# Mixing experts on sixteen small array tiles, loading one image's planes at another place, and a new order in layer 3's first steps

## The chip, the cores and the metric

One Trainium2 chip, and one of its cores. The metric is the device time of one execution in microseconds. A core has a matrix engine (TensorE, PE in the profile, with PEld for its weight loads), a vector engine (VectorE, DVE), a scalar engine (ScalarE, ACT), GpSimd (POOL) and SyncE (SP), which here only starts transfers; sixteen DMA engines move data between the chip's memory (DRAM) and the on-chip memories. TensorE writes its sums into PSUM, eight banks of 128 partitions x 512 fp32 values. Everything is fp32, and TensorE handles each fp32 product in two passes: the profile shows two records for each.

## The reference

Four layers on eight images of 512 channels and 32x32 positions. Layer 0: group norm, eight-head attention, three steps of `h += 0.1*tanh(W h + b)`, a projection and a residual. Layer 1: single-head self-attention with a residual. Layer 2: up- and downsampling with a leaky ReLU between. Layer 3, where most of the change lies, mixes eight sets of expert weights per image and runs a bottleneck with them:

```python
pooled = x.mean(axis=(2, 3))
rw = jax.nn.sigmoid(pooled @ router_w.T + router_b)      # 8 gates for each image
W  = jnp.einsum('be,eoihw->boihw', rw, experts)          # the image's own weights
out = relu(bn(conv1x1(x, W1)));  out = relu(bn(conv3x3(out, W2)))
out = relu(bn(conv1x1(out, W3)) + x)
```

## The kernel before

All 128-row operands are kept as tiles of 128 partitions. Large products are done by seven half-size products (P1, C11, U2, U3, C22, C21, C12), whose operands are sums of quarters made by VectorE (`quarter_sums`). `product` runs them with the banks A in a small PSUM pool and X, Y in the pool `ps_sc`, two buffers of two banks; `in_turn` runs the same seven with one output half after the other, in three banks of the small pool.

The images run one after the other through layers 0 to 2; an image's layer 2 is interleaved with the next image's first products. The last image, number 7, has no next one: beside its layer 2 the kernel runs layer 3 of images 0 and 1 (`lean_images`), a generator named `chain` from which one step is taken at each `fill()`. Images 2 to 7 follow in the main loop of layer 3.

**The early experts.** The gates of images 0 to 6 are known before image 7's layer 0 ends, so `blend_early` mixes their weights there. The experts are laid out as 128 rows (16 groups of 8 experts) by 17,408 columns, cut into 34 pieces of 512. `operators` puts the gates into a block-diagonal 128x128 operand (the rows of `ident`, grouped by `here`, times the gates); each piece is one 128x128x512 product (L310), copied out of PSUM by ScalarE (L316) and stored by GpSimd's queue (L317) in the DRAM tensor `mixed`. One piece is taken at each of the seven parts of the last two inner steps, and three at each part of the last projection. `load_weights` (L1504) reads an image's weights back from there in three loads of 128 rows; `mixed_of` (L236) finds the rows.

**Where the order comes from.** Attention, `last_across`, `last_rows`, `last_columns` and the main loop of layer 3 stand in sections whose order is as written for TensorE, VectorE and ScalarE (in the `last_` ones for SP too). The end of layer 0 with the mixing, and layer 1, are ordered by a scheduler. Each engine takes its instructions in the order that results, and SP its transfers.

**Layer 2 of image 7.** `wide` (L1232) makes columns, stored through `across` and read back as `turned` (`turn`); `fine_passes` runs `up(n)` (L1262), two scaled copies by ScalarE (L1268) and two maxima by VectorE (L1269), then `down(n-1)` (L1280, copies to `sent` L1286, stores `back_u` L1289), and two fills; `turn_back`, `narrow` and `channels` follow. `load_z(1)` (L1466), image 1's planes, stands behind `turn(1)` in `last_across`.

**Layer 3.** `first` is the 1x1 convolution c1 (L1631) and its ReLU into `rim`; `spread` makes sums of its columns; `second` runs c2 (L1573) and c3 (L1667), whose result VectorE adds to the image's planes (L1670), ScalarE finishes (L1673) and SP stores. `transform_weights` turns the 3x3 weights into sums, one ScalarE operation (L1521) and three on VectorE (L1522 to L1524) an image. `blend_last` mixes image 7's weights beside the main loop.

Wide temporary tiles (`tmp` with 1024 columns) rotate through six buffers, `big_tile` through seven.

Of the kernel before, what the change touches and what calls it, by code (L numbers as in the profile page):

```python
# [36 lines left out]
NR = P // NE  # L37
WE = NE * WX
# [19 lines left out]
def tile_sequence(ctx: ExitStack, tc: tile.TileContext, a: dict, out: bass.AP, shifted: bool):  # L58
# [156 lines left out]
    def late_loads():  # L215
# [10 lines left out]
        "early": const.tile([P, B, NR], F32, name="blend_early"),  # L226
# [3 lines left out]
    nc.gpsimd.memset(blend["early"], 0.0)  # L230
    mixed = {
        "early": spill.tile([EARLY * NR, WE], F32, name=f"mixed_{run}", tag="mixed"),
# [3 lines left out]
    def mixed_of(b):  # L236
        rows = mixed["last"] if b == EARLY else mixed["early"][ts(b, NR), :]
        return rows.rearrange("g (p c) -> (g p) c", c=WX)

    class Router:  # L240
# [34 lines left out]
        def operator(self, to):  # L275
            for _ in self.operators(to):
                pass

        def operators(self, to):
            here = ident.rearrange("p (g e) -> p g e", e=NE)  # L280
            for b in range(self.n):
                t = tmp(f"here_{self.name}_{b}")[:, 0:P].rearrange("p (g e) -> p g e", e=NE)
                gate = rw[:, self.images, :][:, b, :].unsqueeze(1).to_broadcast([P, NR, NE])
                nc.vector.tensor_tensor(t, here, gate, ALU.mult)
                nc.vector.tensor_reduce(to[:, b, :], t, AX.X, ALU.add)
                yield

    PIECES = WE // HALF
    BLOCK = CC * S // HALF

    def blend_early():
        rows = EARLY * NR
        op = blend["early"].rearrange("p b g -> p (b g)")
        tiles = []

        def load():
            at = len(tiles) * BLOCK * HALF
            n = min(BLOCK * HALF, WE - at)
            if n > 0:
                t = big_tile(f"experts_{len(tiles)}", [P, BLOCK * HALF])  # L300
                nc.sync.dma_start(t[:, 0:n], a["experts"][:, at : at + n])
                tiles.append(t)

        for _ in range(2):
            load()
        yield
        for i in range(PIECES):
            ps = bank(ps_tp, f"mix_{i}")
            n, at = divmod(i, BLOCK)
            nc.tensor.matmul(  # L310
                ps, op, tiles[n][:, ts(at, HALF)], start=True, stop=True
            )
            if at == BLOCK - 1:
                load()
            t = tmp(f"mix_{i}")
            nc.scalar.copy(t[0:rows, :], ps[0:rows, :])  # L316
            nc.gpsimd.dma_start(mixed["early"][:, ts(i, HALF)], t[0:rows, :])  # L317
            yield

    def blend_last():  # L320
        per = -(-PIECES // 4)
# [3 lines left out]
        def load(t):  # L325
            tiles[t] = big_tile(f"last_experts_{t}", [P, 4, 2 * HALF])
            for c in range(4):
                n = min(2, per - 2 * t, PIECES - per * c - 2 * t)
                if n > 0:
                    at = (per * c + 2 * t) * HALF  # L330
                    nc.sync.dma_start(
                        tiles[t][:, c, 0 : n * HALF], a["experts"][:, at : at + n * HALF]
                    )

        def counts(t):
            return [max(0, min(2, per - 2 * t, PIECES - per * c - 2 * t)) for c in range(4)]

        n_tiles = -(-per // 2)
        load(0)
        yield  # L340
        for t in range(n_tiles):
# [4 lines left out]
            for i in range(2):  # L346
# [12 lines left out]
                if i == counted[0] - 1:  # L359
                    for c in range(4):  # L360
                        n = counted[c] * HALF
                        at = (per * c + 2 * t) * HALF
# [449 lines left out]
    def early_router():  # L812
        router = Router(0, EARLY)
        router.sums()
        yield
        router.logits()
        router.gates()
        yield
        yield from router.operators(blend["early"])

    def layer0(b, q, k, v, w):
# [202 lines left out]
        for it in (1, 2):  # L1024
# [189 lines left out]
    class Layer2:  # L1214
# [37 lines left out]
        def up(self, e, i):  # L1252
# [88 lines left out]
        def fine_passes(self, fill=lambda: None):  # L1341
            order = [(e, i) for e in range(2) for i in range(4)]
            for n in range(len(order) + 1):
                if n < len(order):
                    self.up(*order[n])
# [5 lines left out]
                fill()  # L1351
                fill()
# [62 lines left out]
    def last_across(b, chain, eT, v, inv, y):  # L1415
        two = Layer2(b)
        act, dve = nc.scalar.copy, nc.vector.tensor_copy
        with tc.manual_schedule(engines=hand):
# [13 lines left out]
            zs[1] = load_z(1)  # L1432
        return two

    def last_rows(two, chain, loads):
# [8 lines left out]
        with tc.manual_schedule(engines=hand):  # L1444
            two.fine_passes(fill)
# [58 lines left out]
    def load_weights(b):  # L1504
        wt = pool3.tile([P, WU], F32, tag="weights", bufs=3, name=f"weights_{b}")
        u = wt[:, C : C + 12 * P].rearrange("p (y s o) -> p y s o", y=3, s=4)
        for dst, first, last in (
# [4 lines left out]
            src = mixed_of(b)[:, first:last]  # L1512
            if first == C:
                src = src.rearrange("p (y s o) -> p y s o", y=3, s=3)
            nc.sync.dma_start(dst, src)
        return wt

    def transform_weights(b):
        u = wts[b][:, C : C + 12 * P].rearrange("p (y s o) -> p y s o", y=3, s=4)
        g0, g1, g2, even = (u[:, :, i, :] for i in range(4))  # L1520
        nc.scalar.mul(g1, g1, 0.5)  # L1521
        nc.vector.tensor_add(even, g0, g2)  # L1522
        nc.vector.scalar_tensor_tensor(even, even, 0.5, g1, ALU.mult, ALU.subtract)
        nc.vector.scalar_tensor_tensor(g1, g1, 2.0, even, ALU.mult, ALU.add)  # L1524
# [116 lines left out]
    def second(b):  # L1641
# [17 lines left out]
        yield  # L1659
# [163 lines left out]
```

## Time and profile before

| what | value |
|---|---|
| median of 3 runs | 3565.41 us (3562.42 to 3566.73) |
| the profiled execution | 3565.32 us, of which the span from first to last instruction is 3563.5 |
| TensorE clock granted | 0.997 of full |
| inner steps and projection of image 7, with the mixing | about 3075 to 3202 us of the span |
| layer 1 of image 7 and the products behind it | 3202 to 3298 us |
| layer 2 of image 7 beside layer 3 of images 0 and 1 | 3298 to 3404 us |
| layer 3 of images 2 to 7 | 3404 to 3563 us |
| mean of DMA over the span | 101 GB/s; 339 GB/s from 3346 to 3404 us |

How to read the profile: a row of it names the source line, the engine, the operation, out<-in by the program's tile names, the shapes and the count. A "c" is a bank of one of layer 3's convolutions, told apart by the line. Idle time of an engine is put down to what ended it, in brackets or behind an arrow. Busy TensorE means that a product was under way, also when it waited inside a group.

### The profile page before, as it was taken

How to read it: one execution, taken by the hardware profiler on the slowest of the kernel's cores; microseconds unless marked ns; L12 is line 12 of the kernel's file. 1: busy time of each engine (PE TensorE's matmuls, PEld its weight loads, DVE VectorE, ACT ScalarE, POOL GpSimd, SP SyncE). 2: the span in 40 equal slices, each digit the busy share in tenths (PEclk: the TensorE clock that was granted, in tenths of full speed). 3: DMA queues.
4: the chain of work that ended last, by engine and by line, in shares of the span. 5: the costliest groups of instructions: out<-in, count | busy, mean ns of one | idle time of the engine just before them, and what ended most of it. 6: DMA issues, size and time to landing. Idle time of an engine off the chain costs nothing.

```text
span 3563.5 us, 47886 instructions
## 1 busy us (share of the span) xinstructions
PE 3520.5 (99%) x19445; PEld 1753.9 (49%) x19445; DVE 2321.2 (65%) x3130; ACT 1318.2 (37%) x1740; POOL 102.3 (3%) x140
## 2 busy tenths in 40 slices
PE   8999999999999999999999999999999999999898
PEld 4336643474435743474534753465434744347243
DVE  4787568765676557775677657775687657755444
ACT  0632345223542246323452236323452235431443
POOL 4100000000000000000000000000000000010000
PEclk9999999999999999999999999999999999999999
DMA  5102341115211351014411242023411152332783
GB/s 204 40 30 86 106 169 43 44 55 163 107 35 65 116 181 27 35 67 136 145 36 65 87 143 79 30 86 107 169 42 45 60 165 98 117 107 74 248 310 126
DMA packets 149032, 360.86 MB, mean 101 GB/s; under 512 B 17792, under 2 KB 92560, under 8 KB 142144
## 3 DMA queue, kind: packets, MB, share of 16 engines
q1 hardware_dynamic: 144336, 338.56, 28.2%
q0 software_dynamic: 4320, 18.87, 1.5%
q8 instruction: 155, 2.54, 0.3%
q14 instruction: 77, 0.63, 0.1%
q10 hardware_dynamic: 144, 0.26, 0.0%
HBM read 226.55 MB, written 118.49 MB: 97 GB/s over the span
## 4 chain that ended last, share of the span: by engine, by line
PE 97%; DVE 1%; DMA 1%; ACT 0%; issue 0%; POOL 0%; DVEq 0%; ACTq 0%; POOLq 0%; SPq 0%
PE scores L851 12%; PE av L896 12%; PE inl_X L564 7%; PE av_X L1203 5%; PE inl_Y L564 5%; PE inl_A L564 5%; PE av_A L1203 3%; PE av_Y L1203 3%; PE v_X L564 3%; PE proj_X L564 2%; PE k_X L622 2%; PE c L1573 2%; PE q_X L622 2%; PE v_X L622 2%; PE up L1262 2%; PE v_Y L564 2%
## 5 line engine op out<-in xcount | busy, mean ns | idle before, releaser
L870 ACT ACTIVATE e<-scores 128x1024 f32<-128x1024 f32 x504 | 516.6, 1025 | 395.5 <-PE scores L851 368.9
L851 PE MATMUL scores<-q,k 64*64 64x512 f32 x4096 | 530.7, 591 | 0.0
L896 PE MATMUL av<-e,v 64*64 64x512 f32 x4096 | 528.7, 589 | 0.0
L880 DVE TENSOR_TENSOR accs<-accs,e 128x1024 f32<-128x1024 f32 x240 | 294.2, 1226 | 49.1 <-ACT e L870 45.3
L896 PEld LDWEIGHTS av<-e,v 64*64 64x64 f32 x4096 | 156.5, 133 | 282.3 <-issue 274.1
L851 PEld LDWEIGHTS scores<-q,k 64*64 64x64 f32 x4096 | 152.8, 133 | 289.9 <-issue 255.6
L564 PE MATMUL inl_X<-T_hf,w_inl 128*128 128x512 f32 x576 | 261.6, 593 | 0.3 <-DVE inl_U L718 0.3
L1269 DVE TENSOR_TENSOR fine<-up,fine 128x1024 f32<-128x1024 f32 x128 | 150.8, 1220 | 122.4 <-ACT fine L1268 122.4
L1268 ACT ACTIVATE fine<-up 128x1024 f32<-128x1024 f32 x128 | 124.0, 1020 | 171.8 <-PE up L1262 170.0
L707 ACT ACTIVATE inl_U<-inl_U,inl_b 128x512 f32<-128x512 f32 x96 | 66.9, 718 | 298.6 <-DVE inl_U L722 298.6
L564 PEld LDWEIGHTS inl_X<-T_hf,w_inl 128*128 128x128 f32 x576 | 108.7, 190 | 138.9 <-issue 111.3
L564 PE MATMUL inl_A<-hf,w_inl 128*128 128x512 f32 x384 | 174.7, 597 | 0.0
L917 DVE RECIPROCAL inv<-av 128x256 f32<-128x256 f32 x80 | 139.0, 1746 | 0.0
L718 DVE TENSOR_TENSOR inl_U<-inl_X,inl_P 128x512 f32<-128x512 f32 x96 | 61.8, 686 | 109.0 <-PE inl_X L564 109.0
L878 DVE TENSOR_TENSOR accs<-e,e 128x1024 f32<-128x1024 f32 x48 | 59.7, 1243 | 99.1 <-ACT e L870 80.1
L1203 PE MATMUL av_A<-v,eT 128*128 128x256 f32 x512 | 122.6, 383 | 0.0
L564 PEld LDWEIGHTS inl_A<-hf,w_inl 128*128 128x128 f32 x384 | 71.5, 190 | 96.8 <-issue 86.3
L1203 PE MATMUL av_X<-v,eT 128*128 128x256 f32 x512 | 113.9, 381 | 0.0
L1240 ACT COPY wide<-wide 128x1024 f32<-128x1024 f32 x62 | 59.8, 1015 | 139.6 <-PE wide L1232 139.6
L1092 ACT ACTIVATE eT<-scores 128x512 f32<-128x512 f32 x128 | 66.1, 602 | 115.4 <-PE scores L391 115.4
L1203 PEld LDWEIGHTS av_X<-v,eT 128*128 128x128 f32 x512 | 96.6, 190 | 19.3 <-DVE av_U L1177 6.5
L880 DVE TENSOR_TENSOR acc<-acc,e 128x1024 f32<-128x1024 f32 x80 | 96.9, 1211 | 8.4 <-ACT e L870 7.6
(398 smaller groups left out, 5536.9 us busy)
## 6 DMA issues: line engine op xcount, KB each, us to landing
x<-in_x_dram SPq DMA_DIRECT2D x64, 512.0 KB, 6.5
across_u<-wide SPq DMA_DIRECT2D x128, 256.0 KB, 3.7
turned<-across_u SPq DMA_DIRECT2D x64, 512.0 KB, 5.7
back_u<-sent SPq DMA_DIRECT2D x256, 128.0 KB, 2.2
back<-back_u SPq DMA_DIRECT2D x32, 1024.0 KB, 7.0
w_v<-stored_u_v SPq DMA_DIRECT2D x14, 1792.0 KB, 11.6
out_dram<-z SPq DMA_DIRECT2D x31, 512.0 KB, 3.1
spill_u<-z SPq DMA_DIRECT2D x28, 512.0 KB, 3.3
```

Source lines behind the costliest of these rows:

```text
L564: nc.tensor.matmul(dst, lhs, rhs, start=(opens and s == 0 and cc == 0), stop=(cc == 1 and s == rows), skip_group_check=True,)
L622: nc.tensor.matmul(dst, lhs, rhs, start=(what in opens and s == 0 and cc == 0), stop=(cc == 1 and s == rows), skip_group_check=True,)
L851: nc.tensor.matmul(ps[r][rows[c]], k[rows[r], oc, jc * P + c * HD : jc * P + c * HD + HD], q[rows[r], oc, ts(sh, HALF)], start=True, stop= ...
L870: nc.scalar.activation(e, pair, AF.Exp, scale=HD ** -0.5)
L880: nc.vector.tensor_add(accs[g], accs[g], e)
L896: nc.tensor.matmul(avs[g][r][rows[c]], v[rows[r], jc, ts(2 * oc + c, HD)], e[rows[r], ts(c, HALF)], start=(jc == 0), stop=(jc == SC - 1),)
L917: nc.vector.reciprocal(copies[g][:, at], totals[g][:, at])
L1203: nc.tensor.matmul(ps[:, ts(s, QR)], left[:, j, at : at + P], right[:, j, :], start=(what in ("P1", "U2", "C22") and s == 0 and j == 0), s ...
L1262: nc.tensor.matmul(pairs[g // 2][HD * s : HD * s + HD, ts(g % 2, HALF)], up_v[part, :], self.turned[e][part, first : first + 2, :], start= ...
L1268: nc.scalar.mul(t, ps, 0.2)
L1269: nc.vector.tensor_max(t, ps, t)
L1573: nc.tensor.matmul(ps, wts[b][:, at : at + P], spreads[b][:, i, 16 * ky : 16 * ky + HALF], start=(start and ky == 0), stop=(stop and ky == ...
```

## The change

It has these parts:

- `blend_early` works on array tiles of 32x32. The operand is 128x32 now: `folded` sums `ident` over its four 32-wide parts, and `operators` makes 4 rows' gates for 8 images in 32 columns. Four pieces, a quarter of all pieces apart, are multiplied at a time: row group r (32 partitions) of piece c goes through tile (r, c) into bank r, rows 32c to 32c+31. The four banks are the two buffers of `ps_sc`. ScalarE copies each bank out; per 1024 columns there are sixteen stores of 28 rows, half by SP and half by GpSimd. Three tiles of experts are loaded ahead.
- The mixing runs beside the last projection only, one round at each of its parts, and that projection uses `in_turn`.
- `mixed` has another row order, so `load_weights` makes four loads of 32 rows for each one of before, for images 0 to 6.
- `load_z(1)` stands before `wide(1, 1)`.
- In `last_rows` the second maximum of `up` comes after the first fill.
- `transform_weights` is six GpSimd operations.
- In `second` a yield stands one step earlier, and an output's last ScalarE operation and its store follow one step later (`closed`).
- In the main loop the router's gates come after c2's second part.

```diff
     blend = {
-        "early": const.tile([P, B, NR], F32, name="blend_early"),
+        "early": const.tile([P, B, NL], F32, name="blend_early"),
...
+    folded = const.tile([P, NL, NE], F32, name="folded")
+    nc.vector.tensor_reduce(
+        folded.rearrange("p l e -> p (l e)"), ident.rearrange("p (r k) -> p k r", k=W),
+        AX.X, ALU.add,
+    )
...
-        "early": spill.tile([EARLY * NR, WE], F32, name=f"mixed_{run}", tag="mixed"),
+        "early": spill.tile([P, WE], F32, name=f"mixed_{run}", tag="mixed"),
...
     def mixed_of(b):
-        rows = mixed["last"] if b == EARLY else mixed["early"][ts(b, NR), :]
-        return rows.rearrange("g (p c) -> (g p) c", c=WX)
+        if b == EARLY:
+            return [(slice(0, P), mixed["last"].rearrange("g (p c) -> (g p) c", c=WX))]
+        rows = [mixed["early"][W * r + NL * b : W * r + NL * b + NL, :] for r in range(4)]
+        return [
+            (slice(W * r, W * r + W), row.rearrange("g (p c) -> (g p) c", c=WX))
+            for r, row in enumerate(rows)
+        ]
...
+    PER = -(-PIECES // 4)
+
+    def counts(t):
+        return [max(0, min(2, PER - 2 * t, PIECES - PER * c - 2 * t)) for c in range(4)]
+
+    def load_experts(name, t):
+        tile = big_tile(f"{name}_{t}", [P, 4, 2 * HALF])
+        for c, n in enumerate(counts(t)):
+            if n > 0:
+                at = (PER * c + 2 * t) * HALF
+                nc.sync.dma_start(tile[:, c, 0 : n * HALF], a["experts"][:, at : at + n * HALF])
+        return tile
...
     def blend_early():
-        for i in range(PIECES):
-            ps = bank(ps_tp, f"mix_{i}")
-            n, at = divmod(i, BLOCK)
-            nc.tensor.matmul(
-                ps, op, tiles[n][:, ts(at, HALF)], start=True, stop=True
-            )
...
-            t = tmp(f"mix_{i}")
-            nc.scalar.copy(t[0:rows, :], ps[0:rows, :])
-            nc.gpsimd.dma_start(mixed["early"][:, ts(i, HALF)], t[0:rows, :])
-            yield
+        op = blend["early"].rearrange("p b l -> p (b l)")
+        rows, n_tiles, ahead = EARLY * NL, -(-PER // 2), 3
+        tiles = {t: load_experts("experts", t) for t in range(ahead)}
         yield
+        for t in range(n_tiles):
+            counted = counts(t)
+            dst = [tmp(f"mix_{t}_{r}", S) for r in range(4)]
+            for i in range(counted[0]):
+                pairs = [
+                    ps_sc.tile([P, S], F32, tag="scores", name=f"mix_{t}_{i}_{p}") for p in range(2)
+                ]
+                banks = [pairs[r // 2][:, ts(r % 2, HALF)] for r in range(4)]
+                last = W * sum(n > i for n in counted)
+                for r in range(4):
+                    for c in range(4):
+                        if counted[c] > i:
+                            nc.tensor.matmul(
+                                banks[r][W * c : W * c + W, :], op[W * r : W * r + W, :],
+                                tiles[t][W * r : W * r + W, c, ts(i, HALF)],
+                                start=True, stop=True,
+                            )
+                for r in range(4):
+                    nc.scalar.copy(dst[r][0:last, ts(i, HALF)], banks[r][0:last, :])
+                if i == counted[0] - 1:
+                    for r in range(4):
+                        for c, n in enumerate(counted):
+                            at = (PER * c + 2 * t) * HALF
+                            if n:
+                                (nc.gpsimd if c % 2 else nc.sync).dma_start(
+                                    mixed["early"][W * r : W * r + rows, at : at + n * HALF],
+                                    dst[r][W * c : W * c + rows, 0 : n * HALF],
+                                )
+                    if t + ahead < n_tiles:
+                        tiles[t + ahead] = load_experts("experts", t + ahead)
+                yield
...
             for i, _ in enumerate(parts):
                 for _ in range(2 if i < 4 else 0):
                     next(operators, None)
-                next(mixing, None)
...
-        for _ in product(f"proj_{b}", w["proj"], hf, t, residual(f"proj_{b}", x)):
-            for _ in range(3):
+        if b + 1 < B:
+            all_of(product(f"proj_{b}", w["proj"], hf, t, residual(f"proj_{b}", x)))
+        else:
+            for _ in in_turn(f"proj_{b}", w["proj"], hf, t, residual(f"proj_{b}", x)):
                 next(mixing, None)
...
             for ps, t in zip(pairs, fine):
                 nc.scalar.mul(t, ps, 0.2)
-                nc.vector.tensor_max(t, ps, t)
+                if not apart or t is fine[0]:
+                    nc.vector.tensor_max(t, ps, t)
+            return lambda: nc.vector.tensor_max(fine[1], pairs[1], fine[1])
...
                 if n < len(order):
-                    self.up(*order[n])
+                    second = self.up(*order[n], apart)
...
                 fill()
+                if apart and second is not None:
+                    second()
                 fill()
...
+            zs[1] = load_z(1)
             two.wide(1, 1, y, (act, dve))
             next(chain)
             two.wide(1, 0, y, (act, dve))
             two.turn(1)
-            zs[1] = load_z(1)
...
-            src = mixed_of(b)[:, first:last]
-            if first == C:
-                src = src.rearrange("p (y s o) -> p y s o", y=3, s=3)
-            nc.sync.dma_start(dst, src)
+            for part, src in mixed_of(b):
+                src = src[:, first:last]
+                if first == C:
+                    src = src.rearrange("p (y s o) -> p y s o", y=3, s=3)
+                nc.sync.dma_start(dst[part], src)
...
-        nc.scalar.mul(g1, g1, 0.5)
-        nc.vector.tensor_add(even, g0, g2)
-        nc.vector.scalar_tensor_tensor(even, even, 0.5, g1, ALU.mult, ALU.subtract)
-        nc.vector.scalar_tensor_tensor(g1, g1, 2.0, even, ALU.mult, ALU.add)
+        nc.gpsimd.tensor_add(even, g0, g2)
+        nc.gpsimd.tensor_scalar(even, even, 0.5, None, ALU.mult)
+        nc.gpsimd.tensor_scalar(g1, g1, 0.5, None, ALU.mult)
+        nc.gpsimd.tensor_sub(even, even, g1)
+        nc.gpsimd.tensor_add(g1, g1, g1)
+        nc.gpsimd.tensor_add(g1, g1, even)
...
         nc.vector.tensor_add(one, odd, one)
+        yield
         nc.scalar.activation(h2[:, ts(1, HALF)], one, AF.Relu, bias=bn[1][1], scale=bn[1][0])
-        yield
...
+        def closed(oc):
+            dst = zs[b][:, oc, :]
+            nc.scalar.activation(dst, dst, AF.Relu, bias=bn[2][1][:, oc : oc + 1])
+            nc.sync.dma_start(out[b, ts(oc, P), :], dst)
...
-            nc.scalar.activation(dst, dst, AF.Relu, bias=bias)
-            nc.sync.dma_start(out[b, ts(oc, P), :], dst)
+            if oc:
+                closed(oc - 1)
             yield
+        closed(CC - 1)
...
-            else:
+            c2(b, odd, 3, True, True)
+            if b == LEAN:
                 router.logits()
                 router.gates()
-                router.operator(blend["last"])
-            c2(b, odd, 3, True, True)
+                router.operator("last")
```

More of the change, by code (lines that the diff above doesn't have):

```diff
@@ L37 @@
 NR = P // NE
+NL = W // NE
 WE = NE * WX
@@ L230, in tile_sequence @@
     nc.gpsimd.memset(blend["early"], 0.0)
+    here = {"last": ident.rearrange("p (g e) -> p g e", e=NE)}
+    folded = const.tile([P, NL, NE], F32, name="folded")
[3 more added lines that the diff above has]
+    )
+    here["early"] = folded
     mixed = {
-        "early": spill.tile([EARLY * NR, WE], F32, name=f"mixed_{run}", tag="mixed"),
+        "early": spill.tile([P, WE], F32, name=f"mixed_{run}", tag="mixed"),
         "last": spill.tile([NR, WE], F32, name=f"mixed_last_{run}", tag="mixed_last"),
@@ L273, in gates, with operator, operators @@
             nc.vector.reciprocal(at, at)
-        def operator(self, to):
-            for _ in self.operators(to):
-                pass
-        def operators(self, to):
-            here = ident.rearrange("p (g e) -> p g e", e=NE)
+        def operator(self, which):
+            for _ in self.operators(which):
+                pass
+        def operators(self, which):
+            mask, to = here[which], blend[which]
+            n = mask.shape[1]
             for b in range(self.n):
-                t = tmp(f"here_{self.name}_{b}")[:, 0:P].rearrange("p (g e) -> p g e", e=NE)
-                gate = rw[:, self.images, :][:, b, :].unsqueeze(1).to_broadcast([P, NR, NE])
-                nc.vector.tensor_tensor(t, here, gate, ALU.mult)
+                t = tmp(f"here_{self.name}_{b}")[:, 0 : n * NE]
+                t = t.rearrange("p (g e) -> p g e", e=NE)
+                gate = rw[:, self.images, :][:, b, :].unsqueeze(1).to_broadcast([P, n, NE])
+                nc.vector.tensor_tensor(t, mask, gate, ALU.mult)
                 nc.vector.tensor_reduce(to[:, b, :], t, AX.X, ALU.add)
@@ L288, in tile_sequence @@
     PIECES = WE // HALF
-    BLOCK = CC * S // HALF
-    def blend_early():
[L292 to L305, printed above, removed]
-        yield
-        for i in range(PIECES):
-            ps = bank(ps_tp, f"mix_{i}")
-            n, at = divmod(i, BLOCK)
-            nc.tensor.matmul(
-                ps, op, tiles[n][:, ts(at, HALF)], start=True, stop=True
-            )
-            if at == BLOCK - 1:
-                load()
-            t = tmp(f"mix_{i}")
-            nc.scalar.copy(t[0:rows, :], ps[0:rows, :])
-            nc.gpsimd.dma_start(mixed["early"][:, ts(i, HALF)], t[0:rows, :])
-            yield
+    PER = -(-PIECES // 4)
@@ L320, in blend_last @@
     def blend_last():
-        per = -(-PIECES // 4)
         op = blend["last"].rearrange("p b g -> p (b g)")
@@ L325, in load @@
         def load(t):
[L326 to L338, printed above, removed]
+            tiles[t] = load_experts("last_experts", t)
+        n_tiles = -(-PER // 2)
         load(0)
@@ L361, in blend_last @@
                         n = counted[c] * HALF
-                        at = (per * c + 2 * t) * HALF
+                        at = (PER * c + 2 * t) * HALF
                         if n:
@@ L818, in early_router @@
         yield
-        yield from router.operators(blend["early"])
+        yield from router.operators("early")
     def layer0(b, q, k, v, w):
@@ L1250, in turn, with up @@
                 nc.sync.dma_start(t[:, ts(i, 4), :], src[:, ts(i, 4), :])
-        def up(self, e, i):
+        def up(self, e, i, apart=False):
             n = 4 * e + i
@@ L1339, in channels, with fine_passes @@
                 nc.sync.dma_start(spilled[b][ts(cc, P), :], t)
-        def fine_passes(self, fill=lambda: None):
+        def fine_passes(self, fill, apart=False):
             order = [(e, i) for e in range(2) for i in range(4)]
             for n in range(len(order) + 1):
+                second = None
                 if n < len(order):
-                    self.up(*order[n])
+                    second = self.up(*order[n], apart)
                 if n:
@@ L1444, in last_rows @@
         with tc.manual_schedule(engines=hand):
-            two.fine_passes(fill)
+            two.fine_passes(fill, apart=True)
     def last_columns(b, two, chain, loads):
@@ L1659, in second @@
         yield
+        def closed(oc):
+            dst = zs[b][:, oc, :]
+            nc.scalar.activation(dst, dst, AF.Relu, bias=bn[2][1][:, oc : oc + 1])
+            nc.sync.dma_start(out[b, ts(oc, P), :], dst)
         for oc in range(CC):
-            scale, bias = bn[2][0][:, oc : oc + 1], bn[2][1][:, oc : oc + 1]
-            dst = zs[b][:, oc, :]
-            apart = dst.rearrange("p (n i) -> p i n", i=2)
+            scale = bn[2][0][:, oc : oc + 1]
+            apart = zs[b][:, oc, :].rearrange("p (n i) -> p i n", i=2)
             at = C + 12 * P + oc * P
```

## The prediction

> **What bounds the kernel now.** I read the page first, then the chain of waits by stage, then the timeline of the two stages that the diff touches. The page says one thing for the whole run:
>
> ```profile
> PE 3520.5 (99%) x19445; PEld 1753.9 (49%) x19445; DVE 2321.2 (65%) x3130; ACT 1318.2 (37%) x1740; POOL 102.3 (3%) x140
> PE 97%; DVE 1%; DMA 1%; ACT 0%; issue 0%; POOL 0%; DVEq 0%; ACTq 0%; POOLq 0%; SPq 0%
> ```
>
> TensorE is the path almost everywhere, so the change can gain in two ways only: fewer TensorE microseconds, or the few percent in which TensorE waits. Both exist. The tile view of mix gives the first, 34 products of two passes each (68 records) on the full array; the view of busy time by stage and the chain of waits give the second (the stage's columns are time, PE, PEld, DVE, ACT and POOL busy, TensorE clock, DMA share, GB/s).
>
> ```profile
> L310 PE MATMUL mix<-experts,blend_early x68: 592/592/677, 3103.8 to 3201.7; 128*128 128x512 f32 x68
> L316 ACT COPY mix<-mix x34: 564/586/590, 3104.9 to 3202.3; 112x512 f32<-112x512 f32 x34
> ...
> 3298.00:3346.00 48.00, 39.36 (x256) 12.62 (x260) 23.98 (x30) 20.35 (x27) 0.00 (x0) 0.93 0.60 197
> 3346.00:3404.00 58.00, 49.80 (x266) 19.61 (x251) 29.83 (x40) 25.93 (x34) 0.00 (x0) 0.94 0.93 339
> ...
> 3311.98 7.57 DMA z<-spill_u
> ```
>
> The two stage rows say that from 3298 to 3404 us TensorE is idle 8.6 + 8.2 us, and that DMA is 93% busy in the second. TensorE's own timeline there shows where (the brackets are the wait and what ended it):
>
> ```profile
> 3310.53 1.98 PE L1631 MATMUL c<-z,weights 128*128 128x512 f32 x4
> 3319.69 3.75 PE L1631 MATMUL c<-z,weights 128*128 128x512 f32 x4 [7.17 <-DMA z<-spill_u]
> 3323.38 1.11 PE L1262 MATMUL up<-turned,up_v 32*64 32x512 f32 x16
> ...
> 3343.43 1.12 PE L1667 MATMUL c<-h,weights 128*128 128x512 f32 x2 [0.33 <-ACT h L1657]
> ...
> 3352.53 1.98 PE L1667 MATMUL c<-h,weights 128*128 128x512 f32 x4 [3.82 <-DVE z L1670]
> ...
> 3361.10 3.55 PE L1631 MATMUL c<-z,weights 128*128 128x512 f32 x4 [2.61 <-DVE z L1670]
> ...
> 3391.05 5.40 PE L1667 MATMUL c<-h,weights 128*128 128x512 f32 x8 [1.13 <-DVE z L1670]
> ```
>
> The reader is to see one long DMA stall (image 1's planes) and a row of short ones that VectorE ends.
>
> [...] This trace has no 16-tile group; its 8-tile groups (up, 32x64) end in 1.11 us for 16 records, so tiles do run together. [...] an up group starts 0.19 us later than its predecessor's 0.43 us records alone would give. [...] GpSimd at about half VectorE's speed for two inputs: here 1268 ns (L1112) against 686 ns, 128x512. [...]
>
> **1. The early experts.** Removed: 34 products at 0.858 us (two records 0.43 us apart), 29.2 us, all on the path. Image 6 shows that nothing hid under them: from its last inner step's inl_A (2713.27) to proj_A (2737.30) are 24.0 us, image 7 with seven products takes 30.0.
>
> Added: nine rounds of 16 small products (12 in the last two), each round in two halves of 8, because each PSUM pair takes two row groups. In the built order most halves stand apart, with a projection step between. Nearest row: up and dn, 8 tiles each, 1.03 us from first weight load to the next group's. 18 x 1.03 = 18.5 us. Seven pairs of halves are adjacent; where no copy separates them they may overlap by up to 0.85 us each: I take half of it, -3. Eleven returns to the full array at 0.19 us: +2.1. The first product of the new order that needs T_hf's sums (proj_X) can't run before 5.3 to 7.1 us after the inner step's end (at 3159.5 before; the sums end at 3164.8 and 3166.6); before, 3.4 us of proj_A, 2.7 of mix and 3.4 of proj_A covered this, now 1.7 and three halves: +2. Scalar copies: 36 x 0.586 = 21.1 us against 34 x 0.586 = 19.9, but a half must wait for the copies of the half before the last; by hand through the order that costs a few tenths per tile, +1. Sum 20.6, so -8.6, call it **-9**. Bounds: fully overlapped rounds at 1.1 us give -16. The other bound is the store side: 76 stores instead of 34, half of them on SP, 112 KB each. The copies rotate through six wide buffers (one held by the projection), so from the second tile on each copy waits for the stores of a tile ago; I count 4 us of room. Stores landed in 2.7 us before (224 KB); at 6 us, four tiles lose 2 us each and the part gives 0. The experts' loads (8.2 us) finish in time: three tiles are asked for at 3064, used from about 3148.
>
> **2. Image 1's planes.** load_z(1) moves ahead of wide(1,1), so SP reaches it after turn(0)'s issue (3296.4) and the buffer's release (the end of av_Y, 3298.1), not at 3311.98. Four 512 KB loads landed in 9.0 us, so by 3308; needed about 3311. What it moves past: eight stores of across and turned_1's four loads, which follow it by up to 5 us; turned_1 is needed at up(4), 3337 before and about 3327 then, and would be there by 3321. Gain: 3312.51 to 3323.38 is 10.87 us for a step of 1.79 (the late step also ran at a lower clock): **-9.1**.
>
> **3. Layer 3's first steps.** transform_weights leaves ScalarE and VectorE (0.52 + 0.55 + 0.56 + 0.56 us an image) for six GpSimd operations: at 1.27 and 1.49 us per 512 elements, 384 cost 0.95 and 1.1, about 6 us. GpSimd has nothing behind it but its own next weights, and each is needed 20 us or more after landing: nothing on the path. At the start it frees the copies of wide(1,0): gap 1.14 and up's 1.66 instead of 1.11, about **-1**. In image 0's c3 the stalls are 0.33 + 3.82 + 2.61, and 3.55 - 1.98 = 1.57 of slow step: 8.3 us. VectorE per pass is now 2 x 1.22 + 4 x 0.745 + (0.68 in half of them) = 5.4 to 6.1 us beside TensorE's 2.06 + 2 x 1.9 = 5.9; the second maximum moved behind the first c3, and closed() moved a step back, let them alternate, with VectorE just the limit. I leave 2.8 us: **-5.5**. In image 1's c3: 0.54 + 1.13 and 5.40 - 3.6 = 1.8 us, of which the weights operation (VectorE idle 3.50 us there for ScalarE L1521) goes: **-2.5**. The router's move and the fold of the identity: about 0, no stall stood there; so the early gates, smaller operations beside attention.
>
> **Added on SP.** Each early image's weights come as twelve loads, not three: 63 more issues at about 0.42 us. The build gives SP eight DMA semaphores in turn, so a load also waits for the one eight before it. For images 0 and 1 there is room (3242 to 3277). Image 2's stand before sent_4's stores in SP's queue, and sent_6's copy on ScalarE waits for those (it already waited 1.1 us at 3368.8). I take **+3** here, between 0 (shorter loads land sooner) and +8. In the last images SP's 28 transfers a period of 27 us at 0.45 us fit.
>
> Sum: -9 - 9.1 - 1 - 5.5 - 2.5 + 3 = -24. The profiled execution is 3565.3 us (span 3563.5), the median 3565.4, so both give **3541**.
>
> **Rivals.** (a) The stores govern: SP and GpSimd queues hold the copies, part 1 gives nothing; 3565.4 - 15 = 3550. For it: halves gated in order and transfers of 8 us in the same rings; against: 2.7 us landings. (b) Layer 3's stage becomes DMA-bound: share 0.93 leaves little to compress, the gains of part 3 vanish behind SP and only 9 - 3 of the planes remain with part 1: 3550. For it: the 339 GB/s; against: much of that traffic (z3, z4, the last experts) is prefetch. (c) Slower: the sixteen tiles stall between ScalarE's copies (L340) and the 28-partition stores. Each of the four tile changes costs the landing time less 4 us; the other gains (15, and 9 here) are used up at 6 us a tile, and from a landing time of about 12 us (experts' loads took 8.2, up to 11) the kernel is over 7 us slower: at 12.5, 3565.4 - 24 + 4 x 8.5 = 3575. (d) The tiles do not overlap beyond two: each half 2.2 us, 18 x 1.17 = +21, near no change, 3562.
>
> **How the numbers follow.** Forecast 0.55; (a) 0.15; (b) 0.15; (c) 0.09; (d) 0.06, half of it within 0.2%. About 0.2% (7 us) is what a measurement can tell from none. Faster 0.85, same 0.06, slower 0.09. The likeliest case's own range: -37 (part 1 at -16, part 3 with nothing left and SP at 0) to -15, so 3528 to 3550; with the worse ends of (a) and (b), where SP takes 8 instead of 3 or the stores a little more, 3528 to 3558.
>
> **What would show it.** Right: some 270 mix records in place of 68, groups of 16 ending within 1.2 us, the time from inl's end to v_A about 45 us after it; c at L1663 without a z wait; 3298 to 3404 shortened by about 15. Wrong: mix copies that wait for a DMA of mixed, sent copies that wait for back_u longer than 3 us, or up waiting for turned_1. The forecast is wrong if the stores take over 6 us to land or if the weights' twelve loads hold SP past image 2.

## The result, and the profile after

| kernel | median of all runs shown | lowest to highest | ratio to before |
|---|---|---|---|
| before | 3565.24 us (22 runs) | 3562.15 to 3566.73 | |
| changed | 3570.97 us (22 runs) | 3565.82 to 3574.76 | 1.0016, interval 1.0009 to 1.0022 |

The change makes the kernel slower by 0.16%; the forecast was 3541. The profiled execution has a span of 3569.3 us against 3563.5. The page of the changed kernel has nearly the same TensorE time as before, more GpSimd, and less TensorE in the chain of waits (95% against 97%). First come busy microseconds by engine, then the chain's shares:

```profile
PE 3520.5 (99%) x19649; PEld 1745.7 (49%) x19649; DVE 2320.6 (65%) x3107; ACT 1314.7 (37%) x1734; POOL 160.3 (4%) x190
...
PE 95%; DMA 2%; DVE 2%; issue 0%; SPq 0%; ACT 0%; POOL 0%; DVEq 0%; ACTq 0%; POOLq 0%
```

The expert mixing, by tile, answers to the 68 full-array records of before:

```profile
L334 PE MATMUL mix<-experts,blend_early x272: 584/612/1057, 3150.7 to 3194.6; 32*32 32x512 f32 x136
...
L340 ACT COPY mix<-mix x36: 574/591/617, 3152.4 to 3196.5; 128x512 f32<-128x512 f32 x28, 96x512 f32<-96x512 f32 x8
...
DMA to landing us min/median/max: 2.5/3.6/6.5
```

Busy time of each engine in three stretches of the changed kernel (columns as in the prediction: time, PE, PEld, DVE, ACT, POOL, TensorE clock, DMA share, GB/s):

```profile
3150.00:3199.50 49.50, 44.47 (x326) 13.01 (x325) 22.46 (x32) 21.22 (x40) 17.91 (x36) 0.93 0.60 191
3199.50:3301.00 101.50, 97.68 (x465) 75.42 (x463) 57.62 (x76) 17.93 (x30) 22.32 (x17) 0.98 0.25 73
3301.00:3395.00 94.00, 79.95 (x445) 26.75 (x444) 42.53 (x49) 39.15 (x51) 6.57 (x6) 0.91 0.77 255
```

The reader is to see a clock of 0.93 in the mix stage, 22.3 us of GpSimd in layer 1 (5.7 us in the kernel before), and 14 us of idle TensorE still there behind it (94.00 less 79.95).

To find where the time went I cut every profile at the same TensorE steps. "Mix" runs from attention's last step to the first v_A product of layer 1, "layer 1" from there to the last `wide`, "lean" from there to the first group of sixteen c1 records of the main loop, "main" to the end of the last product. All kernels of this study stand in the table; the stages are those of one profiled execution each, the last column is the median of each kernel's runs.

| kernel | mix | layer 1 | lean | main | sum | median |
|---|---|---|---|---|---|---|
| before | 125.2 | 98.9 | 100.8 | 153.5 | 478.5 | 3565.2 |
| changed | 122.1 | 104.6 | 100.8 | 157.3 | 484.8 | 3571.0 |
| a_dve | 122.0 | 98.9 | 100.3 | 156.6 | 477.8 | 3563.0 |
| a_four | 123.1 | 104.6 | 100.9 | 157.3 | 485.8 | 3572.3 |
| a_both | 118.2 | 98.9 | 100.9 | 155.9 | 473.8 | 3563.8 |
| b_z1 | 125.2 | 98.9 | 91.4 | 153.5 | 469.1 | 3556.2 |
| a_noapart | 121.6 | 103.0 | 89.5 | 157.4 | 471.5 | 3559.4 |
| b_mix | 117.6 | 98.9 | 103.0 | 155.6 | 475.2 | 3566.1 |
| b_first3 | 125.2 | 98.9 | 97.1 | 153.5 | 474.7 | 3562.0 |
| c_best | 121.9 | 98.9 | 89.2 | 156.9 | 466.9 | 3553.7 |
| d_load | 120.4 | 98.9 | 90.2 | 154.4 | 463.9 | 3550.3 |
| d_old | 125.2 | 98.9 | 86.4 | 153.5 | 464.0 | 3551.8 |
| d_busy | 120.9 | 98.9 | 90.6 | 157.2 | 467.6 | 3554.5 |
| e_fill | 117.5 | 98.9 | 89.9 | 154.5 | 460.7 | 3548.1 |

For the changed kernel the stages differ from before by -3.1, +5.8, 0.0 and +3.8 us: a small gain, two losses at places where the prediction had none, and a stage in which gains and losses cancel. By its own terms the prediction had -9, 0, -15.1 and 0 there.

### The profile page after: what moved, and what is told of

Read it like the earlier page. It is cut to its first block, busy times and chain, and to the rows that moved or that the text cites. A ratio compares the mean times of both kernels' runs of the same rounds, so it can differ in the third digit from the quotient of the medians.

```text
span 3569.3 us, 48520 instructions
## 1 busy us (share of the span) xinstructions
PE 3520.5 (99%) x19649; PEld 1745.7 (49%) x19649; DVE 2320.6 (65%) x3107; ACT 1314.7 (37%) x1734; POOL 160.3 (4%) x190
## 4 chain that ended last, share of the span: by engine, by line
PE 95%; DMA 2%; DVE 2%; issue 0%; SPq 0%; ACT 0%; POOL 0%; DVEq 0%; ACTq 0%; POOLq 0%
PE scores L874 12%; PE av L919 12%; PE inl_X L587 7%; PE av_X L1227 5%; PE inl_Y L587 5%; PE inl_A L587 5%; PE av_Y L1227 3%; PE av_A L1227 3%; PE v_X L587 3%; PE k_X L645 2%; PE c L1605 2%; PE q_X L645 2%; PE v_X L645 2%; PE proj_X L587 2%; PE v_Y L587 2%; PE up L1286 2%
## 5 line engine op out<-in xcount | busy, mean ns | idle before, releaser
L1294 DVE TENSOR_TENSOR fine<-up,fine 128x1024 f32<-128x1024 f32 x120 | 141.7, 1220 | 112.7 <-ACT fine L1292 112.6
L1136 POOL TENSOR_TENSOR seen<-seen,acc 128x512 f32<-128x512 f32 x16 | 20.3, 1271 | 2498.2 <-DVE acc L1128 2497.6
```

## The experiments

**Theories.** A: GpSimd's six operations slow VectorE's sums in layer 1. B: the twelve loads hold SP's queue. C: the planes' load holds the stores of `across` and gives its gain back. E, formed after the first four runs: the second maximum behind the fill stands behind work that has nothing to do with it. F: the last experts come late. G: TensorE's clock falls in the mix stage because TensorE sits idle between the first rounds. Rivals stand in each expectation.

**a_dve: GpSimd's part undone.**

```diff
-        nc.gpsimd.tensor_add(even, g0, g2)
-        nc.gpsimd.tensor_scalar(even, even, 0.5, None, ALU.mult)
...
-        nc.gpsimd.tensor_add(g1, g1, even)
+        nc.scalar.mul(g1, g1, 0.5)
+        nc.vector.tensor_add(even, g0, g2)
+        nc.vector.scalar_tensor_tensor(even, even, 0.5, g1, ALU.mult, ALU.subtract)
+        nc.vector.scalar_tensor_tensor(g1, g1, 2.0, even, ALU.mult, ALU.add)
```

> The changed kernel with image weights transformed by ScalarE and VectorE (four operations) again instead of six on GpSimd. Theory A (GpSimd's six operations slow VectorE's two-operand sums while both run in layer 1): the stage from v_A to wide(1,1), 101.5 us with the change, falls by about 5 us to 96, av_X loses its 3.8 us wait; in layer 3's first steps some of the stalls by z come back (2 to 4 us), and the whole is 3566 to 3569, 2 to 5 us below the changed kernel. Rival (the layer 1 loss comes from loads and stores of the new mixing, not from GpSimd): that stage stays at 101 us, the whole gets 2 to 4 us slower than the changed kernel.

Measured: 3563.0 us, ratio 0.9994 (0.9986 to 1.0003); layer 1 took 98.9 us, the value of before to a tenth. Theory A holds. The whole fell by 8.0 us, more than expected: the stalls by z did not come back, and the lean stage stayed at 100.3 us. VectorE's timeline in the changed kernel (start, busy time, line, operation, shapes, count):

```profile
3251.10 3.15 DVE L1178 TENSOR_TENSOR S<-S,eT 128x1024 f32<-128x1024 f32 x2
...
3255.69 3.46 DVE L1178 TENSOR_TENSOR eT<-eT,eT 128x1024 f32<-128x1024 f32 x2
3259.06 2.72 DVE L1178 TENSOR_TENSOR v<-v 128x512 f32<-128x512 f32 x2
```

The same operations in a_dve:

```profile
3250.21 2.35 DVE L1178 TENSOR_TENSOR S<-S,eT 128x1024 f32<-128x1024 f32 x2
...
3253.68 2.35 DVE L1178 TENSOR_TENSOR eT<-eT,eT 128x1024 f32<-128x1024 f32 x2
3255.95 1.28 DVE L1178 TENSOR_TENSOR v<-v 128x512 f32<-128x512 f32 x2
```

GpSimd in the changed kernel, at the same time:

```profile
3251.19 1.97 POOL L1551 TENSOR_TENSOR weights<-weights 128x384 f32<-128x384 f32 x1
3253.15 2.13 POOL L1553 TENSOR_SCALAR weights<-weights 128x384 f32<-128x384 f32 x1
```

And TensorE in the changed kernel:

```profile
3269.22 8.85 PE L1227 MATMUL av_X<-v,eT 128*128 128x256 f32 x32 [3.82 <-DVE av_U L1199]
```

The three pairs shown are slowed by 0.8, 1.1 and 1.4 us. VectorE reaches the sum that frees av_X's bank late, so TensorE waits 3.82 us for it and then, at a clock of 0.81, takes 8.85 us for a step that takes 7.07 in a_dve. The two together are 5.6 of the 5.8 us. Nothing was queued behind GpSimd, as the prediction said; the loss came through the engine beside it.

**a_four and a_both: four loads of weights in place of twelve.** Each row group's 1408 columns come in one load; the sums go to a place of their own. a_both has the edit of a_dve too.

```diff
-        for dst, first, last in (
...
-                nc.sync.dma_start(dst[part], src)
+        for part, src in mixed_of(b):
+            nc.sync.dma_start(wt[part, 0:WX], src)
...
```

> The changed kernel with each early image's weights fetched by four loads (32 rows of all 1408 columns) instead of twelve. Theory B (twelve loads hold SP's queue, each waiting for the one eight before it): back_u's stores of image 2's stage are issued about 9 us earlier (3355 instead of 3364), ScalarE's sent copies wait under 2 us instead of 7 and 7, the stage from wide(1,1) to the first main loop step falls from 103.7 to 94 to 99, the whole is 3561 to 3566. Rival (DMA bandwidth of that stage, 339 GB/s, is the limit and not the queue): the stores start earlier but land as late, the stage stays within 2 us and the whole at 3569 to 3571.

> Both edits: the weights transformed by ScalarE and VectorE, and four loads of weights. If the two losses are separate they add: about 5 in layer 1 and 5 to 9 in the next stage less 2 to 4 for returning stalls: 3558 to 3564. If the lean stage's gain hangs on GpSimd having the weights (stalls by z return in full), 3564 to 3568.

Measured: a_four 3572.3 us, 1.0018 (1.0012 to 1.0025), the lean stage 100.9; a_both 3563.8, 0.9998 (0.9989 to 1.0006), 100.9. Theory B falls for the changed kernel: fewer loads alone do not free its lean stage. The rival's picture fits better. `back_u`'s stores were issued sooner (3357.5 us against 3364.6), but ScalarE's copy still waited 6.39 us for one to land (7.33 in the changed kernel), and TensorE waited 4.31 us for weights. What four loads are worth where the stage is not held otherwise was not run. a_both is no faster than a_dve.

**b_z1: image 1's planes alone.**

```diff
+            zs[1] = load_z(1)
             two.wide(1, 1, y, (act, dve))
...
-            zs[1] = load_z(1)
```

> The kernel before with only the load of image 1's planes moved ahead of wide(1,1). Prediction's step: the 7.2 us stall and the slow step go, -9, so 3556. Theory C (its 2 MB stands in front of the stores of across, which hold the wide buffers that fine needs, so up waits for fine and the gain is partly given back): -3 to -5, 3560 to 3562. Theory that nothing is gained (the wait only moves): 3564 to 3566.

Measured: 3556.2 us, 0.9974 (0.9964 to 0.9983), lean 91.4, so -9.4. The prediction's step is right to 0.3 us and theory C falls. The changed kernel has the same edit and its lean stage is 100.8: the rest of the change costs about nine microseconds there.

**a_noapart and b_first3: the second maximum.** The first is the changed kernel without its late second maximum; the second is b_z1 with the late maximum, `closed` and the router's move.

```diff
-            two.fine_passes(fill, apart=True)
+            two.fine_passes(fill)
```

> The changed kernel with the second maximum of each fine pass back ahead of the fill, in all passes. Theory E (put behind the fill, it stands on VectorE behind the next step's spread sums and what they wait for, so up and dn of passes 2 and 7 wait for fine 3.6, 3.9 and 3.4 us and run slowly after): these waits go, some of the stalls of image 0's c3 (3.8 and 2.2 us in the kernel before) come back; the stage from the last wide to the main loop's first full step falls from 100.8 us to 92 to 97, the whole is 3561 to 3567. Rival (the stage is held by the stores of across behind the planes' load, and by back_u behind twelve loads): up(2) still waits for fine about 3 us and the stage stays at 99 or more, the whole at 3569 to 3572.

> The kernel before with image 1's planes loaded sooner and layer 3's first steps reordered (second maximum behind the fill, closed one step back, the router's move), without GpSimd and without the new mixing. Beside the 3556.2 us of the planes alone: the prediction's step for the order (-5.5 and part of -2.5) gives 3549 to 3551. Theory E gives the c3 stalls back at passes 2 and 7: 3555 to 3560.

Measured: a_noapart 3559.4 us, 0.9984 (0.9975 to 0.9992), lean 89.5: this line alone costs 11.3 us of that stage in the changed kernel. b_first3 3562.0, 0.9990 (0.9982 to 0.9999), lean 97.1 against 91.4 for the planes alone, so the new order as a whole loses 5.7 where it was to gain. Theory E holds for where the time goes, though both sizes were off: a_noapart came out below its range and b_first3 above it. TensorE in the changed kernel:

```profile
3317.10 1.07 PE L1286 MATMUL up<-turned,up_v 32*64 32x512 f32 x4
3321.74 2.00 PE L1286 MATMUL up<-turned,up_v 32*64 32x512 f32 x12 [3.57 <-DVE fine L1295]
...
3369.00 2.41 PE L1306 MATMUL dn<-fine,dn_v 64*32 64x512 f32 x8 [3.85 <-ACT sent L1312]
3374.77 1.93 PE L1306 MATMUL dn<-fine,dn_v 64*32 64x512 f32 x8 [3.36 <-DVE fine L1295]
```

VectorE in the changed kernel at the first of these places:

```profile
3315.03 1.23 DVE L1294 TENSOR_TENSOR fine<-up,fine 128x1024 f32<-128x1024 f32 x1 [3.67 <-ACT fine L1292]
3317.92 0.73 DVE L1595 TENSOR_TENSOR spread<-rim 128x544 f32<-128x544 f32 x1 [1.66 <-ACT rim L1585]
...
3320.47 1.22 DVE L1295 TENSOR_TENSOR fine<-up,fine 128x1024 f32<-128x1024 f32 x1
```

The first maximum is done at 3316.3. The second could follow, but the fill between them brought four sums of `spread`, the first of which waits 1.66 us for `rim` on ScalarE. The maximum runs at 3320.47, and the `up` that needs its PSUM buffer waits. Around 3370 it happens again, in pass 7 (the passes of `fine_passes` are counted from 0), and here a second cause stands behind it. The sums wait for `rim`, and ScalarE makes `rim` only after its copy to `sent`, which waits for one of `back_u`'s stores; these stand on SP behind image 2's twelve loads of weights:

```profile
3350.19 14.28 SPq L1545 DMA_DIRECT2D weights<-mixed_u  x12
...
3368.36 1.07 ACT L1312 COPY sent<-dn 128x512 f32<-128x512 f32 x2 [7.33 <-DMA back_u<-sent]
```

In the kernel before the loads are three and the wait is 1.11 us:

```profile
3354.18 4.34 SPq L1515 DMA_DIRECT2D weights<-mixed_u  x3
```

TensorE of a_noapart, all its waits of the stage after 3306:

```profile
3342.57 1.98 PE L1704 MATMUL c<-h,weights 128*128 128x512 f32 x4 [1.26 <-DVE z L1707]
...
3350.40 1.98 PE L1663 MATMUL c<-z,weights 128*128 128x512 f32 x4 [1.86 <-DVE z L1707]
...
3362.27 1.59 PE L1306 MATMUL dn<-fine,dn_v 64*32 64x512 f32 x16 [3.88 <-ACT sent L1312]
```

Both waits for `fine` are gone, and of the c3 stalls of before (3.82 and 2.61 us) 1.26 and 1.86 are back. The wait for `sent` stays, so it is not the second maximum's.

**b_mix: the new mixing alone** (the changed kernel with everything else put back, its loads of weights kept).

```diff
-            zs[1] = load_z(1)
             two.wide(1, 1, y, (act, dve))
...
+            zs[1] = load_z(1)
...
-            two.fine_passes(fill, apart=True)
+            two.fine_passes(fill)
...
```

> The kernel before with the new mixing alone (its loads and stores and the twelve loads of weights for each early image with it). If the mixing saves what its stage shows (3 us, up to 7 when TensorE's clock does not fall in it) and costs nothing later: 3558 to 3562. If its loads cost afterwards as in the changed kernel (last experts 3 us late in the main loop, and SP's queue in layer 3's first steps): 3563 to 3568, nothing gained.

Measured: 3566.1 us (3561.9 to 3570.9), 1.0005 (0.9997 to 1.0013). Its profiled execution is one in which TensorE's clock stayed at 1.00: mix 117.6, that is -7.6; then lean +2.2 and main +2.1. So 3.3 us are left in an execution at full clock, and the median shows none of them.

**c_best: what the theories advise.** The weights of images 0 and 1 by ScalarE and VectorE again, GpSimd from image 2 on; the second maximum late in passes 5 and 6 alone, where the fill holds c3.

```diff
-                second = None
+                second, apart = None, n in late
...
-            two.fine_passes(fill, apart=True)
+            two.fine_passes(fill, late=(5, 6))
...
+        if b < LEAN:
+            nc.scalar.mul(g1, g1, 0.5)
...
```

> The changed kernel with the weights of images 0 and 1 transformed by ScalarE and VectorE (later ones on GpSimd), and the second maximum behind the fill in passes 5 and 6 alone, where c3 runs. If theories A and E hold, layer 1 gives 5.8 back and the stage behind it 7 to 10: 3553 to 3559, faster than the kernel before. If the stalls at passes 2 and 7 come from the queues: 3562 to 3566.

Measured: 3553.7 us, 0.9970 (0.9958 to 0.9982): 17 us below the changed kernel, by two edits, and inside the range that theories A and E gave.

**d_old and d_load: is the mixing worth it, and what does it cost later?** d_old is c_best with the mixing, loads and stores of before. d_load is c_best with one block moved.

```diff
-            if b + 2 < B:
-                if b + 3 < B:
-                    zs[b + 2] = load_z(b + 2)
-                    wts[b + 2] = load_weights(b + 2)
...
                 for _ in range(2):
                     next(mixing, None)
+            if b + 3 < B:
+                zs[b + 2] = load_z(b + 2)
+                wts[b + 2] = load_weights(b + 2)
```

> The kernel before with the good parts alone: image 1's planes sooner, closed one step back, the router's move, the second maximum behind the fill in passes 5 and 6, GpSimd for the weights of image 2 and later; the old mixing on the full array. If the new mixing is worth its 3 to 6 us net, this is 3555 to 3558, above c_best (3553.7); if its later costs and the clock's fall eat what it saves, 3547 to 3552.

> The labelled kernel c_best with the loads of planes and weights of the image after next issued behind the mixing's steps of each main loop image instead of ahead of them. Theory F (the last experts' loads stand on SP behind sixteen loads of planes and weights and land after mix_last asks for them, 3.0 us at 3480 in the changed kernel): the wait for last_experts goes, the stage from the first full step of the main loop to the end, 157 us, is 2 to 3 us shorter, the whole 3550 to 3552. Rival (the same bytes through the same DMA engines): the wait moves to z or weights, the whole stays at 3553 to 3555.

Measured: d_old 3551.8 us, 0.9963 (0.9949 to 0.9976); d_load 3550.3, 0.9959 (0.9945 to 0.9972). They differ by 1.5 us and their intervals overlap: even with its loads placed better the new mixing shows no gain here. Theory F holds: main falls from 156.9 to 154.4. SP in the changed kernel:

```profile
3466.74 9.44 SPq L1545 DMA_DIRECT2D weights<-mixed_u  x12
3476.22 1.84 SPq L314 DMA_DIRECT2D last_experts<-in_experts_dram  x4
```

TensorE there:

```profile
3480.60 1.82 PE L376 MATMUL mix_last<-last_experts,blend_last 128*32 128x512 f32 x4
3482.84 1.84 PE L376 MATMUL mix_last<-last_experts,blend_last 128*32 128x512 f32 x4 [0.41 <-DMA last_experts<-in_experts_dram]
```

And TensorE in d_load:

```profile
3462.23 1.06 PE L376 MATMUL mix_last<-last_experts,blend_last 128*32 128x512 f32 x8
```

The experts asked for behind planes and weights land when mix_last already waits: 4.1 us (3480.60 to 3484.68) for a step of 1.06 (1.06 in the kernel before, too). The count of loads alone is not it: a_four issues its four there in 2.08 us and main is still 157.3. The place in SP's queue is. The lean stage of d_load is 3.8 us longer than d_old's. The traces put 2.7 us of it at two waits of TensorE behind the twelve loads: 1.99 us for weights and 3.82 for `sent`, against 0.87 and 2.23 in d_old.

**d_busy and e_fill: the clock.** Of the nine profiled executions with the new mixing other than e_fill, seven have a mean clock of 0.86 to 0.96 in this stage and two (a_both, b_mix) have 1.00; all four with the old mixing have 1.00. The whole runs agree: the changed kernel's go from 3565.8 us at a granted clock of 0.997 to 3574.8 at 0.994. d_busy adds one full product behind each of the first two rounds to c_best; e_fill adds three behind the first round to d_load.

```diff
+                if t == 0 and i == 0:
+                    warm = bank(ps_tp, "warm")
+                    for _ in range(3):
+                        nc.tensor.matmul(
+                            warm, tiles[0][:, 0, 0:P], tiles[0][:, 0, 0:HALF],
+                            start=True, stop=True,
+                        )
```

> c_best with one added full product (two passes, 0.86 us) behind each of the first two rounds of the mixing, written to a bank that nobody reads. Theory G (the idle 1.6 us between the first rounds lets TensorE's clock fall, 0.5 to 0.7 for some ten us, worth 3.5 to 5 us in most executions): the clock stays at 1.00 in the mix stage, that stage is 3 to 4 us shorter than c_best's in spite of the added work, and the times scatter less: 3550 to 3552. Rival (the fall has another cause): clock as before, 1 to 2 us longer, 3554 to 3556.

> The labelled kernel d_load with three added full products (2.6 us) behind the first round of the mixing, written to a bank that nobody reads, so that TensorE has work while the sums for proj_X are made. d_busy's two products left 1.7 us idle there. Theory G (idle time at that place starts the fall of TensorE's clock): idle time at 3150 to 3160 under 0.5 us, clock 1.00 in the mix stage, that stage 2 to 3 us shorter than d_load's, the times closer together than d_load's 7.8 us, median 3547 to 3549. Rival (the fall has another cause, such as the switching between array shapes): the clock still falls, 3550 to 3553.

Measured: d_busy 3554.5 us, 0.9967 (0.9955 to 0.9979), clock 0.96, nothing gained. This is what its rival said; but its first product only moved the idle time, 1.73 us before proj_X, so theory G isn't refuted either. e_fill: 3548.1 us (3546.9 to 3550.0), 0.9954 (0.9940 to 0.9967), clock 1.00, mix 117.5 against d_load's 120.4 although 2.6 us of products were added. TensorE in the changed kernel:

```profile
3150.70 1.68 PE L334 MATMUL mix<-experts,blend_early 32*32 32x512 f32 x32
3153.51 1.04 PE L334 MATMUL mix<-experts,blend_early 32*32 32x512 f32 x2 [1.12 <-ACT mix L340]
3155.08 1.12 PE L645 MATMUL proj_X<-T_hf,w_proj 128*128 128x512 f32 x2 [0.53 <-DVE T_hf L548]
...
3157.61 2.08 PE L645 MATMUL proj_X<-T_hf,w_proj 128*128 128x512 f32 x2
```

And in e_fill:

```profile
3152.14 2.84 PE L342 MATMUL warm<-experts 128*128 128x512 f32 x6
3155.00 1.10 PE L652 MATMUL proj_X<-T_hf,w_proj 128*128 128x512 f32 x2
3156.72 1.12 PE L652 MATMUL proj_X<-T_hf,w_proj 128*128 128x512 f32 x2 [0.62 <-DVE T_hf L555]
```

The product of two proj_X records that takes 2.08 us in the changed kernel takes 1.12 here. e_fill has the lowest median of the study, 17 us below before and 23 below the changed one. All its five runs are below all five of d_old (3551.1 to 3552.7), by 3.7 us in the median: the one sign in this study that the new mixing can beat the old one, though the intervals of the two ratios overlap. For theory G this is support and no proof. The runs of d_load (3546.7 to 3554.5) enclose those of e_fill, and a_both and b_mix have the same two waits as the changed kernel (1.12 and 0.53 us) and kept a clock of 1.00, so these waits alone don't decide. Whether idle time or the thin 32x32 products let the clock fall was not separated: the products that fill the gap add full-size work as well. Not tried: four loads of weights in e_fill, and other stores.

## Why the prediction was wrong

The forecast of -24 became +5.7. The step that failed most is the new order of part 3, next come GpSimd's price of nothing and the two terms that the sum did not have, TensorE's clock and the last experts. By the prediction's own steps:

- **Part 1, -9.** Right about the tiles: at full clock, rounds of 16 products that stand together end in 1.22 us, so rival (d) is out. That two halves overlap by up to 0.85 us was the author's estimate; two halves at 1.03 us less these 1.22 give 0.84. Near in size too where the clock holds (-7.6); the "about 45 us" from the inner step's end to v_A came there (45.1 us in b_mix). Missing was TensorE's clock: where it fell, the stage took 2.8 to 5.5 us longer than in b_mix; with it the stage gave -3.1. Rival (a), the stores, is a small part: ScalarE's copies waited 5.5 us in four waits for them, with landings of 3.6 us in the median where the trace gives one.
- **Part 2, -9.1.** Right: -9.4 in b_z1.
- **Part 3, image 0's -5.5: the step that failed most.** "The second maximum moved behind the first c3" holds for two of the eight passes that have one. In the others the fill is c1 or c2, with `spread` and its wait for ScalarE. The prediction priced the move where the stall was and not at every place where the same line runs: the new order cost +5.7 in b_first3, and this line +11.3 in the changed kernel, in place of a gain. Image 1's -2.5 was right in kind: the changed kernel has no stall left at its c3, while b_first3, without GpSimd, still waits 1.13 us for z there. With the move in passes 5 and 6 alone and GpSimd from image 2 on, lean falls from 91.4 (b_z1) to 86.4 (d_old), 5.0 of the 8 us. The -1 at the start didn't come: `up` waits 1.14 us for `wide` in both kernels.
- **GpSimd, "nothing on the path".** +5.8 in layer 1. The prediction asked what is queued behind GpSimd, and not what runs beside it. Layer 1's sums (L1178, `by_two`) take 3.15 us beside GpSimd for a pair that takes 2.35 without it. Not everything on VectorE was slowed: four operations of L1188, which read the bank of av_A, took 1.65 us in a_dve and in the changed kernel alike, in the latter beside GpSimd (at 3261.71). By what means the two engines hold each other up was not shown. The prediction has GpSimd's speed alone (1268 against 686 ns).
- **Twelve loads, +3 in layer 3's first steps.** About right in size, +2.2 (b_mix) and +3.8 (d_load against d_old), and right in its path: ScalarE's copy to `sent` waited for `back_u`, though 7.33 us, where over 3 was one of the prediction's signs of being wrong. The trace of SP shows why twelve loads hold it for 14.28 us: the third to the eighth each wait for the load eight places ahead to land (of `back` and `z`), 9.6 us in all. a_four shows no gain from fewer loads, but in a stage that the late maximum held.
- **"In the last images SP's 28 transfers fit."** They fit in number, not in order: +2.1 in b_mix and +3.8 in the changed kernel, of which 3.0 at one mix_last step, behind planes and weights in SP's queue.

The rival for the slower side, (c), had the wrong mechanism: no store whose landing the trace gives took longer than 6.5 us.

## What to carry to other kernels

When a line inside a loop is moved to cure a stall in some passes, list what stands before and behind it in every pass, on every engine, and move it only where the list is good. An operation that goes to an idle GpSimd has to be priced by what VectorE runs at that time, not by GpSimd's queue (here +5.8 us in layer 1). A stage that mixes small products with short waits can lose to TensorE's clock what the smaller products save (here 2.8 to 5.5 us at a mean clock of 0.86 to 0.96, of the 7.6 that b_mix saved at 1.00), so look at the granted clock of the stage and not only at its products. Work that nobody needs, put in the gap, may be cheaper than the gap; here five runs and one profile speak for it.

## What the runs showed of the hardware

- Six GpSimd operations of 384 columns, alone 0.83 to 1.17 us each (image 2's first five, from 3364.9 to 3370.2 us, beside an idle VectorE), took 1.19 to 2.13 us beside VectorE's two-operand sums in layer 1, and the sums 1.36 us instead of 0.64 (2.72 and 1.28 the pair). Both sides lose. They do not simply take turns: in the 10.6 us from 3251.1 to 3261.7 VectorE did sums that take 6.95 us in a_dve, and GpSimd six operations that take about 6 us beside an idle VectorE (an estimate from image 2's first five, 5.2 us), 13 us in all.
- TensorE's clock fell to 0.66 for ten microseconds in the changed kernel after waits of only 1.12 and 0.53 us around 32x32 products (the clock stands third from the end in these stretches of busy time):

```profile
3150.00:3155.00 5.00, 3.43 (x36) 0.49 (x34) 4.91 (x9) 3.75 (x7) 0.00 (x0) 1.00 0.55 223
3155.00:3160.00 5.00, 4.92 (x23) 1.19 (x34) 3.31 (x7) 0.00 (x0) 0.00 (x0) 0.66 0.00 0
3160.00:3165.00 5.00, 5.00 (x58) 1.35 (x36) 1.70 (x3) 2.05 (x4) 2.52 (x6) 0.66 0.30 73
3165.00:3170.00 5.00, 4.18 (x49) 1.29 (x23) 2.19 (x3) 1.17 (x2) 1.48 (x4) 1.00 0.78 243
```

In layer 1 the clock was 0.81 behind the wait of 3.82 us (3269.2 to 3278.1). How long a wait is doesn't decide alone: in the kernel before, the clock was 1.00 behind the 3.82 us that end at 3352.5 and 0.54 behind the 2.61 us that end at 3361.1. In the mix stage waits of 1.12 us and less, in d_busy one of 1.73, came with a mean clock of 0.86 to 0.96 in seven of nine executions and with 1.00 in the other two, and with the first one filled the one profiled execution kept 1.00. From which length of a wait on the clock falls was not shown. The times scatter there: d_load's five runs span 7.8 us, e_fill's 3.1.
